# A graph layer's edge loop: 139 fetched columns and 15 fetched rows a chunk instead of 35 columns

## The chip, the cores and the metric

The kernel runs on one core of a Trainium2 chip. The metric is the device time of one execution in microseconds; the kernel before has a median of 4821.73 us over 3 runs.

## The reference

A message-passing layer on a graph of 12,500 nodes (48 values each) and 400,000 edges (32 values each), sorted by destination:

```python
h = jnp.maximum(_layernorm(x, axis=-1), 0.0)
x_i, x_j = h[dst], h[src]
tmp = jnp.concatenate([x_i, x_j, edge_attr], axis=1)      # 48 + 48 + 32
msg = jax.nn.relu(tmp @ W1 + b1) @ W2 + b2                # 128 hidden values
out = x + jax.ops.segment_sum(msg, dst, num_segments=12500)
```

## The kernel before, in words

**Tables.** W1 is split by its three inputs. A first stage (`node_tables`) makes the normalised nodes and from them two tables in DRAM of 12,500 rows of 128 values: `tab_a` (what a node gives as a destination, with the bias) and `tab_b` (what it gives as a source). `tab_b` is also kept transposed in SBUF as `bt`, 128 hidden values by nodes, so that one node's row is one column of `bt`.

**The edge loop** (`windows`) goes over 391 chunks of 1,024 edges, each eight tiles of 128 edges. Because the edges are sorted, a chunk's destinations lie in a window of 80 nodes, so the `tab_a` part and the edge part come from one matmul a tile: `rhs` holds the 80 table rows and 32 rows of W1, `lhs` the one-hot of the destinations and the edges' values (`before`, L400, into the PSUM tile `pre`). The source part has no such order and reaches the sum in one of two ways:

- *Gathered*: POOL issues one indirect DMA a tile (L373), which fetches 128 rows of `tab_b` into the tile `gb`. DVE adds `gb` to `pre` (L425).
- *Turned*: for some tiles, ACT and DVE copy 128 single columns of `bt` into a tile `gt` (L351), at addresses that they load into registers from a list of numbers (`last`); PE then adds `gt` transposed to `pre` by a matmul with the identity (`turned`, L409). 35 columns are copied a chunk (`PARTS`: 3 on DVE, 16 + 16 on ACT), so every 3.7 chunks one tile is complete.

`hidden` then makes the relu on ACT (L432, and L431 for a turned tile) into an SBUF tile `h`; `fold` multiplies `h` with the one-hot `hot` of the destinations (L440), and `add` accumulates the result in SBUF (L455). Every twelve chunks a segment is multiplied with W2 and stored.

**Order.** Each engine takes its instructions in the order in which the loop emits them: in iteration `c` the loads, the one-hots and the gathers of chunk `c` (`prepare`; rhs, lhs and row on SP's queue at L359, L364 and L366), then PE's `before` of chunk `c - 1`, `fold` of `c - 2` and `turned` of `c - 1`, then `hidden` of `c - 1` and `add` of `c - 2`, with the column copies of the parts in between. POOL runs ahead as far as buffers allow: `gb` has six (pool `gp`), and one is free again when DVE's add has read it. `pre` has two buffers in PSUM, `rhs` three in SBUF.

Of the kernel before, what the change touches and what calls it, by code (L numbers as in the profile page):

```python
# [8 lines left out]
F32 = mybir.dt.float32  # L9
I32 = mybir.dt.int32  # L10
AF = mybir.ActivationFunctionType
# [5 lines left out]
P = 128  # L17
N, D, DE, HID, E = 12500, 48, 32, 128, 400000
# [3 lines left out]
NT = E // P  # L22
T = 8
# [20 lines left out]
U8 = mybir.dt.uint8  # L44
# [3 lines left out]


COLS = 1  # L50
END = NT // T


PARTS = (
    (True, 0, 3, 1),
    (False, 3, 16, 4),
    (False, 19, 16, 20),
)
PART = sum(n for _, _, n, _ in PARTS)
BASE = 36  # L60
DVE_PARTS = sum(dve for dve, *_ in PARTS)
BEHIND = len(PARTS) - 1

BT0 = 16512
SEG0 = 121888
SEG_SIZE = 8 * L


SEG, NEXT, SEG2 = 40, 41, 42
PLACE0 = 43  # L70
WIDTH = 44
SLOTS = (NCH + 2 + P - 1) // P
MOST = 32

# [1 line left out]
def tiles_of(first, part):  # L76

    n = (END - first) * part // P
    return [first + (P * (j + 1) + part - 1) // part - 1 for j in range(n)]


BYCOLS = tiles_of(COLS, PART)
TURNED = {c: [j for j, of in enumerate(BYCOLS) if of == c] for c in set(BYCOLS)}


def turned_at(c):

    return ((), (T - 1,), (T // 2 - 1, T - 1))[len(TURNED.get(c, ()))]


def gathered_at(c):

    return [t for t in range(min(T, NT - c * T)) if t not in turned_at(c)]


EPS = 1e-5
# [8 lines left out]
def node_tables(nc, tc, keep, bt, x, ident, w1, b1, tab_a, tab_b, loads, most, check, rest):  # L105
# [5 lines left out]
    ta_v = tab_a[:NPAD, :].rearrange("(p r) h -> p r h", p=P)  # L111
    with ExitStack() as es:
        node = es.enter_context(tc.tile_pool(name="node", bufs=3))
        ps_t = es.enter_context(tc.tile_pool(name="ps_t", bufs=3, space=PSUM))
        ps_n = es.enter_context(tc.tile_pool(name="ps_n", bufs=3, space=PSUM))
        ps_s = es.enter_context(tc.tile_pool(name="ps_s", bufs=1, space=PSUM))
# [68 lines left out]
        def table(j, wt, tv, dve):  # L185

            r0, rb = slices[j]
            rows = wt.shape[0]
            t = node.tile([P, rb, HID], F32, name="tab")
            for g in range(0, rb // 2, 2):  # L190
                n = min(2, rb // 2 - g)
                p_n = ps_n.tile([P, 2, 2 * HID], F32, name="p_n")
                for q in range(n):
                    nc.tensor.matmul(
                        p_n[:, q, :], hts[j][:rows, g + q, :],
                        wt.rearrange("k a h -> k (a h)"), start=True, stop=True,
                    )
                to = t[:, 2 * g : 2 * (g + n), :].rearrange("p r h -> p (r h)")
                of = p_n[:, :n, :].rearrange("p q h -> p (q h)")
                if dve and g % 4:  # L200
                    nc.vector.tensor_copy(to, of)
                else:
                    nc.scalar.copy(to, of)
            nc.sync.dma_start(tv[:, r0 : r0 + rb, :], t)
# [43 lines left out]
def windows(nc, tc, gp, bt, ident, idx, x_t, tab_a, tab_b, dst, edge_t, w1, w2s, b2s, out_t):  # L248
# [3 lines left out]
    with ExitStack() as es:  # L252
# [19 lines left out]
        for _, _, n, at in PARTS:  # L272
# [1 line left out]
                last[:, :, at : at + n], last[:, :, at : at + n], 4, BT0,  # L274
                op0=ALU.mult, op1=ALU.add,
            )
        rows_at = slice(BASE, BASE + 1)
        nc.vector.tensor_scalar(
            last[:, :, rows_at], last[:, :, rows_at], 4 * HID, None, op0=ALU.mult
        )  # L280
        taba8 = tab_a.rearrange("n h -> (n h)").bitcast(U8)

        place = PARTS[0][3] - 1
        for a, b in ((place, SEG2), (NEXT, SEG)):
# [16 lines left out]
            rhss.append(rhs)  # L301
        st = {}
        gts = {}

        def group(c):

# [15 lines left out]

        def node(n):
            return n.with_bounds(min_val=0, max_val=N - 1)

        regs = {}

# [25 lines left out]
        def prepare(c):  # L353
            n = min(T, NT - c * T)
            at = c * CE
            base, = numbers(c, BASE, 1, mybir.EngineType.SP)
            rhs = rhss[c % 3]
            base = base.with_bounds(min_val=0, max_val=4 * HID * (N - 1))
            nc.sync.dma_start(  # L359
                rhs.bitcast(U8)[:W, :],  # L360
                taba8[bass.ds(base, 4 * HID * W)].rearrange("(w h) -> w h", w=W),
            )
            lhs = ld.tile([P, CE], F32, name="lhs")
            nc.sync.dma_start(lhs[W:K, : n * P], edge_t[:, at : at + n * P])  # L364
            row = ld.tile([W, CE], I16, name="row")
            nc.sync.dma_start(  # L366
                row[:, : n * P],
                dst[at : at + n * P].rearrange("(o e) -> o e", o=1).to_broadcast([W, n * P]),
            )
            st[c] = dict(n=n)  # L370
            gb = gp.tile([P, T, HID], F32, name="gb")
            for t in gathered_at(c):
                nc.gpsimd.indirect_dma_start(  # L373
                    out=gb[:, t, :], out_offset=None, in_=tab_b[:, :],
                    in_offset=bass.IndirectOffsetOnAxis(
                        ap=srci[:, c * T + t : c * T + t + 1], axis=0
                    ),
                )

            deg = degs[c % 3]  # L380
            nc.vector.tensor_scalar(  # L381
                lhs[:W, : n * P], row[:, : n * P], bw[:, c : c + 1], None,
                op0=ALU.is_equal, op1=ALU.add, accum_out=deg[:, :1],
            )
            load(c, 0)
            columns(c, 0)
            hot = wp.tile([P, T, W], F32, name="hot")
            nc.vector.tensor_tensor(  # L388
                hot[:, :n, :], wnum.unsqueeze(1).to_broadcast([P, n, W]),
                rel[:, c * T : c * T + n].unsqueeze(2).to_broadcast([P, n, W]), op=ALU.is_equal,  # L390
            )
            st[c].update(rhs=rhs, lhs=lhs, gb=gb, deg=deg, hot=hot)
# [18 lines left out]
        def hidden(c):  # L411
            s = st[c]
            n, pre = s["n"], s["pre"]
            h = wp.tile([P, T, HID], F32, name="hid")
            two = len(turned_at(c)) == 2
            half = T // 2

            def added(x, to):

                if not two:  # L420
                    return x[:, :to, :]
                return x.rearrange("p (b t) h -> p b t h", b=2)[:, :, : half - 1, :]

            to = n - len(turned_at(c))
            nc.vector.tensor_add(added(h, to), added(pre, to), added(s["gb"], to))  # L425
            if two:
                nc.scalar.activation(
                    h[:, half - 1 :: half, :], pre[:, half - 1 :: half, :], AF.Relu
                )
            elif to < n:  # L430
                nc.scalar.activation(h[:, to, :], pre[:, to, :], AF.Relu)  # L431
            nc.scalar.activation(added(h, to), added(h, to), AF.Relu)  # L432
            s["h"] = h

        def fold(c):
# [53 lines left out]
        with tc.manual_schedule():  # L489
            for c in range(NCH + 2):  # L490
                if c < NCH:
                    prepare(c)
                if c >= NCH:
                    load(c, 0)
                    columns(c, 0)
                for part in range(1, DVE_PARTS - 1):
                    load(c, part)
                    columns(c, part)
                if 0 <= c - 1 < NCH:
                    before(c - 1)  # L500
                if 0 <= c - 2 < NCH:
                    fold(c - 2)
                if 0 <= c - 1 < NCH:
                    turned(c - 1)

                g, k = group(c - 2)
                if k == GQ - 3 or c == NCH - 1:
                    segment_load(g)
                if g > 0 and k < L // BLK:
                    segment_sum(g - 1, k, BLK)  # L510
                if g > 0 and k == STORE:
                    segment_store(g - 1, L)
                columns(c, DVE_PARTS)
                for part in range(DVE_PARTS + 1, BEHIND):
                    load(c, part)
                    columns(c, part)
                if 0 <= c - 1 < NCH:
                    hidden(c - 1)
                if DVE_PARTS > 1:
                    load(c, DVE_PARTS - 1)  # L520
                for part in range(BEHIND, len(PARTS)):
                    load(c, part)
                    columns(c, part)
                load(c + 1, DVE_PARTS)
                if 0 <= c - 2 < NCH:
                    add(c - 2)
                    if k == GQ - 1:
                        segment_next(g)
                if DVE_PARTS > 1:
                    columns(c, DVE_PARTS - 1)  # L530
                if c == NCH + 1:
                    segment_sum(g, 0, END_L)
                    segment_store(g, END_L)

                if c < PIECES:
                    s = slice(c * PIECE, (c + 1) * PIECE)
                    nc.sync.dma_start(out_t[:, s], x_t[:, s])
# [126 lines left out]
def tile_gnn_preln(  # L664
# [27 lines left out]
    nc = tc.nc  # L692
# [28 lines left out]
    for k in range(3):  # L721
        deg = const.tile([W, P], F32, name=f"deg{k}")
        nc.gpsimd.memset(deg, 0.0)
        degs.append(deg)
    gp = ctx.enter_context(tc.tile_pool(name="gp", bufs=6))

    with tc.tile_pool(name="keep", bufs=1) as keep, tc.tile_pool(
        name="ps_c", bufs=1, space=PSUM
# [146 lines left out]
```

## Time and profile before

| | |
|---|---|
| median of 3 runs (4817.93 to 4830.65) | 4821.73 us |
| profiled execution, its own time | 4847.12 us |
| its span | 4845.3 us |
| mean granted TensorE clock | 0.614 |
| tiles gathered (L373) | 3,019 of 3,125 |
| columns copied on ACT, on DVE (L351) | 12,404, 1,164 |
| moved by DMA | 367.73 MB, 76 GB/s |

The profile is one execution. A group's row gives the source line, the engine, the operation, out<-in by the program's names with the shape, the count, then the busy time, the mean duration of one in ns, and the idle time of the engine just before these instructions with what ended most of it. "issue" is idle time that ended without any wait that the profile shows; "remote" is a release whose origin it does not show. In the timeline a row is a start, a duration, and a run of like instructions.

### The profile page before, as it was taken

The numbers are of one execution on the slowest core, as the hardware profiler recorded it, in microseconds if no ns is written. First come the engines' busy times: TensorE is split into PE (matmuls) and PEld (weight loads), VectorE is DVE, ScalarE is ACT, GpSimd is POOL, SyncE is SP. The second block draws the span as 40 slices with busy tenths as digits, with TensorE's granted clock in tenths as the row PEclk, the third lists the DMA queues.
The fourth block names the chain that finished last, engine by engine and source line by source line (L and its number), as shares of the span: only waits on it lengthen the run. The fifth ranks groups of instructions, "written<-read, shape, count | busy, mean of one in ns | idle before, by whom it ended". The sixth has DMA issues, their size and how long they took to land. (4 is left out here: it accounts for less than half of the span.)

```text
span 4845.3 us, 55629 instructions
## 1 busy us (share of the span) xinstructions
PE 2962.1 (61%) x14064; PEld 2628.5 (54%) x14064; DVE 1534.8 (32%) x3366; ACT 1944.3 (40%) x12976; POOL 2895.0 (60%) x3047
## 2 busy tenths in 40 slices
PE   5565565555667555665556757666566655665656
PEld 3555564455556555655555656555455555554545
DVE  4333323332333232333323333332233332323333
ACT  3344343443334343443443444343344343434443
POOL 5466565565656566665656666656666665656663
PEclk7756656666555655556656565655655566656566
DMA  3422222222222222222222222222222222222222
GB/s 123 145 72 75 75 71 72 73 73 72 75 68 77 72 73 71 76 73 71 76 71 73 77 73 75 73 71 75 73 72 76 72 74 72 76 69 76 74 71 60
DMA packets 199966, 367.73 MB, mean 76 GB/s; under 512 B 69362, under 2 KB 101636, under 8 KB 198356
## 3 DMA queue, kind: packets, MB, share of 16 engines
q0 software_dynamic: 96640, 198.07, 16.4%
q1 hardware_dynamic: 102736, 165.92, 11.5%
q8 instruction: 115, 1.88, 0.2%
q14 instruction: 215, 1.76, 0.1%
q10 hardware_dynamic: 260, 0.10, 0.0%
HBM read 344.35 MB, written 22.07 MB: 76 GB/s over the span
## 5 line engine op out<-in xcount | busy, mean ns | idle before, releaser
L373 POOL DMA_INDIRECT gb<-tab_b,srci x3019 | 2873.3, 952 | 1898.0 <-DVE seg L455 953.0
L351 ACT COPY gt<-bt 128x1 f32 x12404 | 1495.6, 188 | 1985.4 <-issue 1957.3
L400 PE MATMUL pre<-rhs,lhs 112*128 112x128 f32 x6250 | 1357.6, 386 | 866.3 <-issue 655.1
L400 PEld LDWEIGHTS pre<-rhs,lhs 112*128 112x128 f32 x6250 | 1240.2, 292 | 1052.9 <-issue 849.9
L440 PE MATMUL p_g<-hot,hid 128*128 128x80 f32 x6250 | 1210.5, 366 | 691.2 <-ACT hid L432 312.9
L440 PEld LDWEIGHTS p_g<-hot,hid 128*128 128x128 f32 x6250 | 1156.3, 280 | 742.8 <-ACT hid L432 351.3
L425 DVE TENSOR_TENSOR hid<-pre,gb 128x1024 f32<-128x1024 f32 (+1 forms) x391 | 461.4, 1180 | 1727.0 <-issue 1357.5
L432 ACT ACTIVATE hid<-hid 128x1024 f32<-128x1024 f32 (+1 forms) x391 | 400.3, 1024 | 423.3 <-DVE hid L425 318.2
L381 DVE TENSOR_SCALAR_CACHE_REDUCE lhs<-row,bw 80x1024 f32<-80x1024 int16 x391 | 495.4, 1267 | 9.3 <-DMA row<-in_dst 9.3
L455 DVE TENSOR_TENSOR seg<-seg,p_g 128x160 f32 x391 | 122.4, 313 | 977.1 <-remote 824.1
L388 DVE TENSOR_TENSOR hot<-wnum,rel 128x640 f32<-128x640 f32 x391 | 316.1, 809 | 0.0
L443 PE MATMUL p_g<-ident,deg 80*128 80x80 f32 x782 | 213.4, 356 | 139.1 <-issue 138.8
L443 PEld LDWEIGHTS p_g<-ident,deg 80*128 80x128 f32 x782 | 181.1, 278 | 111.8 <-issue 111.4
L483 DVE TENSOR_TENSOR xseg<-xseg,p_f 48x512 f32<-48x512 f32 (+1 forms) x67 | 45.3, 676 | 497.6 <-remote 291.2
L431 ACT ACTIVATE hid<-pre 128x128 f32<-128x128 f32 x106 | 29.4, 278 | 390.0 <-DVE hid L425 273.8
L409 PE MATMUL pre<-ident,gt 128*128 128x128 f32 x212 | 70.1, 399 | 106.0 <-issue 96.1
L409 PEld LDWEIGHTS pre<-ident,gt 128*128 128x128 f32 x212 | 51.7, 282 | 108.8 <-issue 98.5
L482 PE MATMUL p_f<-seg,b2s 1*48 1x512 f32 (+1 forms) x134 | 98.0, 810 | 11.8 <-issue 11.8
L481 PE MATMUL p_f<-seg,w2s 128*48 128x512 f32 (+1 forms) x134 | 98.0, 815 | 11.3 <-issue 10.0
L351 DVE COPY gt<-bt 128x1 f32 x1164 | 103.0, 141 | 0.0
L482 PEld LDWEIGHTS p_f<-seg,b2s 1*48 1x48 f32 x134 | 13.4, 139 | 92.7 <-issue 91.8
L471 DVE MEMSET seg<- 128x944 f32 x64 | 54.1, 845 | 9.3
(66 smaller groups left out, 327.3 us busy)
## 6 DMA issues: line engine op xcount, KB each, us to landing
row<-in_dst SPq DMA_DIRECT2D x390, 160.0 KB
lhs<-in_edge_t SPq DMA_DIRECT2D x390, 128.0 KB
gb<-tab_b,srci POOLq DMA_INDIRECT x3019
rhs<-tab_a SPq DMA_DIRECT2D x391, 40.0 KB
xseg<-in_x_t SPq DMA_DIRECT2D x33, 192.0 KB
out_x<-xseg SPq DMA_DIRECT2D x33, 192.0 KB
tab_b<-tab SPq DMA_DIRECT2D x3, 1280.0 KB
tab_a<-tab SPq DMA_DIRECT2D x3, 1280.0 KB
```

What stands on the lines that cost most here:

```text
L351: copy(gts[of][:, e : e + 1], bt8[:, bass.ds(at, 4)].bitcast(F32))
L373: nc.gpsimd.indirect_dma_start(out=gb[:, t, :], out_offset=None, in_=tab_b[:, :], in_offset=bass.IndirectOffsetOnAxis(ap=srci[:, c * T + t ...
L381: nc.vector.tensor_scalar(lhs[:W, : n * P], row[:, : n * P], bw[:, c : c + 1], None, op0=ALU.is_equal, op1=ALU.add, accum_out=deg[:, :1],)
L388: nc.vector.tensor_tensor(hot[:, :n, :], wnum.unsqueeze(1).to_broadcast([P, n, W]), rel[:, c * T : c * T + n].unsqueeze(2).to_broadcast([P ...
L400: nc.tensor.matmul(pre[:, t, :], s["lhs"][:K, t * P : (t + 1) * P], s["rhs"][:K, :], start=True, stop=t not in turned_at(c),)
L409: nc.tensor.matmul(st[c]["pre"][:, t, :], gts.pop(j), ident, start=False, stop=True)
L425: nc.vector.tensor_add(added(h, to), added(pre, to), added(s["gb"], to))
L432: nc.scalar.activation(added(h, to), added(h, to), AF.Relu)
L440: nc.tensor.matmul(p_g[:, 0, :], s["h"][:, t, :], s["hot"][:, t, :], start=t == 0, stop=t == n - 1)
L443: nc.tensor.matmul(p_g[:, 1, :], s["deg"], ident[:W, :W], start=True, stop=True)
L455: nc.vector.tensor_add(to, to, s["p_g"])
L482: nc.tensor.matmul(p_f[:, :n], b2s[:1, :], seg[:1, 1, s], start=False, stop=True)
```

## The change

- **Columns**: 139 a chunk instead of 35: 63 on DVE (15 + 16 + 16 + 16) and 76 on ACT (16 x 4 + 12), with one load of registers for each group of at most sixteen. About one tile a chunk is turned instead of one in 3.7 chunks; a chunk can have two.
- **Rows**: SP fetches 15 rows of `tab_b` a chunk by DMAs of one row each into a tile `gs`, at addresses from registers. Every 8.5 chunks one tile is complete, and its chunk's DVE add reads `gs` for that tile instead of `gb`. Tiles that are turned or come by rows are not gathered by POOL.
- **The hidden tile**: DVE adds into `pre` in PSUM, and ACT's relu reads all of `pre` from there in one instruction, where DVE wrote to `h` in SBUF and ACT worked in place.
- **Buffers**: eight `gb` tiles instead of six; two buffers for the tables' tile `tab` instead of three.

```diff
 PARTS = (
-    (True, 0, 3, 1),
-    (False, 3, 16, 4),
-    (False, 19, 16, 20),
+    (True, 0, 15, 1),
+    (True, 15, 16, 16),
+    (True, 31, 16, 32),
+    (True, 47, 16, 48),
+    (False, 63, 16, 64),
+    (False, 79, 16, 80),
+    (False, 95, 16, 96),
+    (False, 111, 16, 112),
+    (False, 127, 12, 128),
 )
...
-BASE = 36
+BASE = 140
+RPART = 15
 DVE_PARTS = sum(dve for dve, *_ in PARTS)
-BEHIND = len(PARTS) - 1
+BEHIND = len(PARTS) - 2
...
+BYROWS = tiles_of(ROWS0, RPART)
...
+def single_at(c):
+
+    return (T - 2 if c in TURNED else T - 1) if c in BYROWS else None
+
+
 def gathered_at(c):
 
-    return [t for t in range(min(T, NT - c * T)) if t not in turned_at(c)]
+    return [t for t in range(min(T, NT - c * T)) if t not in turned_at(c) and t != single_at(c)]
...
         node = es.enter_context(tc.tile_pool(name="node", bufs=3))
+        tabs = es.enter_context(tc.tile_pool(name="tabs", bufs=2))
...
-            t = node.tile([P, rb, HID], F32, name="tab")
+            t = tabs.tile([P, rb, HID], F32, name="tab")
...
+        def rows(c, nodes):
+
+            for k, n in enumerate(nodes):
+                e = (c - ROWS0) * RPART + k
+                of = BYROWS[e // P]
+                if of not in gss:
+                    gss[of] = gtp.tile([P, HID], F32, name="gs")
+                n = n.with_bounds(min_val=0, max_val=4 * HID * (N - 1))
+                nc.sync.dma_start(
+                    gss[of].bitcast(U8)[e % P : e % P + 1, :],
+                    tab8[bass.ds(n, 4 * HID)].rearrange("(o h) -> o h", o=1),
+                )
...
-            base, = numbers(c, BASE, 1, mybir.EngineType.SP)
+            m = max(0, min(RPART, len(BYROWS) * P - (c - ROWS0) * RPART)) if c >= ROWS0 else 0
+            base, *nodes = numbers(c, BASE, 1 + m, mybir.EngineType.SP)
...
-            h = wp.tile([P, T, HID], F32, name="hid")
...
-            nc.vector.tensor_add(added(h, to), added(pre, to), added(s["gb"], to))
-            if two:
-                nc.scalar.activation(
-                    h[:, half - 1 :: half, :], pre[:, half - 1 :: half, :], AF.Relu
-                )
-            elif to < n:
-                nc.scalar.activation(h[:, to, :], pre[:, to, :], AF.Relu)
-            nc.scalar.activation(added(h, to), added(h, to), AF.Relu)
+            at = single_at(c)
+            if at is None:
+                parts = [(added(pre, to), added(s["gb"], to))]
+            else:
+                runs = [(0, half - 1), (half, at)] if two else [(0, at)]
+                parts = [(pre[:, a:b, :], s["gb"][:, a:b, :]) for a, b in runs]
+                parts.append((pre[:, at, :], gss.pop(c)))
+            for of, rows in parts:
+                nc.vector.tensor_add(of, of, rows)
+            h = wp.tile([P, T, HID], F32, name="hid")
+            nc.scalar.activation(h[:, :n, :], pre[:, :n, :], AF.Relu)
...
                 if c < NCH:
                     prepare(c)
+                    rows(c, st[c].pop("rows"))
...
-    gp = ctx.enter_context(tc.tile_pool(name="gp", bufs=6))
+    gp = ctx.enter_context(tc.tile_pool(name="gp", bufs=8))
```

More of the change, by code (lines that the diff above doesn't have):

```diff
@@ L50 @@
 COLS = 1
+ROWS0 = 1
 END = NT // T
 PARTS = (
-    (True, 0, 3, 1),
-    (False, 3, 16, 4),
-    (False, 19, 16, 20),
+    (True, 0, 15, 1),
[7 more added lines that the diff above has]
+    (False, 127, 12, 128),
 )
 PART = sum(n for _, _, n, _ in PARTS)
-BASE = 36
+BASE = 140
+RPART = 15
 DVE_PARTS = sum(dve for dve, *_ in PARTS)
-BEHIND = len(PARTS) - 1
+BEHIND = len(PARTS) - 2
 BT0 = 16512
-SEG0 = 121888
+SEG0 = 131936
 SEG_SIZE = 8 * L
-SEG, NEXT, SEG2 = 40, 41, 42
-PLACE0 = 43
-WIDTH = 44
+SEG, NEXT, SEG2 = 156, 157, 158
+PLACE0 = 159
+WIDTH = 160
 SLOTS = (NCH + 2 + P - 1) // P
@@ L276, in windows @@
             )
-        rows_at = slice(BASE, BASE + 1)
+        rows_at = slice(BASE, BASE + 1 + RPART)
         nc.vector.tensor_scalar(
@@ L280, in windows @@
         )
-        taba8 = tab_a.rearrange("n h -> (n h)").bitcast(U8)
+        tab8, taba8 = (t.rearrange("n h -> (n h)").bitcast(U8) for t in (tab_b, tab_a))
         place = PARTS[0][3] - 1
@@ L303, in windows @@
         gts = {}
+        gss = {}
         def group(c):
@@ L369, in prepare @@
             )
-            st[c] = dict(n=n)
+            st[c] = dict(n=n, rows=nodes)
             gb = gp.tile([P, T, HID], F32, name="gb")
@@ L839 @@
         numbers[COLS : COLS + len(cols), at : at + n] = cols[:, k : k + n]
+    in_rows = [c * T + single_at(c) for c in BYROWS]
+    rows = by_tile[in_rows].reshape(-1)
+    rows = np.pad(rows, (0, -len(rows) % RPART)).reshape(-1, RPART)
+    numbers[ROWS0 : ROWS0 + len(rows), BASE + 1 : BASE + 1 + RPART] = rows
     last = np.ascontiguousarray(numbers.reshape(SLOTS, P, WIDTH).transpose(1, 0, 2))
```

## The prediction

> **What bounds the kernel now.** I read the page first: its busy times, its chain of waits and its costliest groups.
>
> ```profile
> span 4845.3 us, 55629 instructions
> PE 2962.1 (61%) x14064; PEld 2628.5 (54%) x14064; DVE 1534.8 (32%) x3366; ACT 1944.3 (40%) x12976; POOL 2895.0 (60%) x3047
> ...
> issue 6%; PE 6%; another core or an unknown queue 3%; DVE 2%; ACT 1%; DVEq 0%; POOL 0%; DMA 0%; ACTq 0%
> ...
> L373 POOL DMA_INDIRECT gb<-tab_b,srci x3019 | 2873.3, 952 | 1898.0 <-DVE seg L455 953.0
> L351 ACT COPY gt<-bt 128x1 f32 x12404 | 1495.6, 188 | 1985.4 <-issue 1957.3
> ...
> L425 DVE TENSOR_TENSOR hid<-pre,gb 128x1024 f32<-128x1024 f32 (+1 forms) x391 | 461.4, 1180 | 1727.0 <-issue 1357.5
> L432 ACT ACTIVATE hid<-hid 128x1024 f32<-128x1024 f32 (+1 forms) x391 | 400.3, 1024 | 423.3 <-DVE hid L425 318.2
> L381 DVE TENSOR_SCALAR_CACHE_REDUCE lhs<-row,bw 80x1024 f32<-80x1024 int16 x391 | 495.4, 1267 | 9.3 <-DMA row<-in_dst 9.3
> L455 DVE TENSOR_TENSOR seg<-seg,p_g 128x160 f32 x391 | 122.4, 313 | 977.1 <-remote 824.1
> L388 DVE TENSOR_TENSOR hot<-wnum,rel 128x640 f32<-128x640 f32 x391 | 316.1, 809 | 0.0
> ...
> L351 DVE COPY gt<-bt 128x1 f32 x1164 | 103.0, 141 | 0.0
> ```
>
> No engine is full (61% at most), and the chain of waits names almost nothing: its largest part is "issue", time in which an engine had nothing to wait for. So the bound is a state, not an instruction. The waits of POOL say how its two kinds of idle time divide:
>
> ```profile
> POOL gb L373 <- DVE seg L455: 953.0, 217, 8.9
> POOL gb L373 <- issue: 855.9, 2762, 1.7
> ```
>
> Between gathers lies 855.9 / 2762 = 0.31 us, so POOL works at 0.952 + 0.31 = 1.26 us a gather, 3,810 us in all; 217 times it stops, 953.0 / 217 = 4.4 us each. 391 chunks over 217 stops are 1.8 chunks a run. The "seg" named is DVE's work just behind the add L425, which frees a gb buffer: POOL stops because all six are full.
>
> Then the timeline over one such cycle:
>
> ```profile
> 2024.19 0.33 SPq L359 DMA_DIRECT2D rhs<-tab_a  x1
> ...
> 2024.62 0.37 SPq L364 DMA_DIRECT2D lhs<-in_edge_t  x1
> 2025.04 0.41 SPq L366 DMA_DIRECT2D row<-in_dst  x1
> ...
> 2025.78 0.95 POOL L373 DMA_INDIRECT gb<-tab_b,srci  x1 [4.55 <-DVE seg L455]
> 2026.66 2.93 ACT L351 COPY gt<-bt 128x1 f32 x29
> ...
> 2026.85 0.27 DVE L351 COPY gt<-bt 128x1 f32 x3
> 2027.03 0.94 POOL L373 DMA_INDIRECT gb<-tab_b,srci  x1 [0.30 <-issue]
> ...
> 2030.04 0.38 ACT L351 COPY gt<-bt 128x1 f32 x3 [0.44 <-issue]
> ...
> 2030.63 3.70 PE L400 MATMUL pre<-rhs,lhs 112*128 112x128 f32 x16
> ...
> 2043.29 0.95 POOL L373 DMA_INDIRECT gb<-tab_b,srci  x1 [0.30 <-issue]
> 2043.53 0.37 PE L400 MATMUL pre<-rhs,lhs 112*128 112x128 f32 x1 [1.73 <-issue]
> 2044.20 0.19 ACT L351 COPY gt<-bt 128x1 f32 x1 [0.51 <-issue]
> ...
> 2047.01 0.93 ACT L351 COPY gt<-bt 128x1 f32 x9 [0.50 <-issue]
> ...
> 2048.72 0.94 POOL L373 DMA_INDIRECT gb<-tab_b,srci  x1 [4.48 <-DVE seg L455]
> ```
>
> At 2026.66 ACT makes 29 copies in 2.93 us, 0.101 us each. From 2030.04 on, 4.3 us after POOL's restart, it starts single copies with half a microsecond of "issue" before each, and PE does the same a little later (2043.53: one matmul after 1.73 us of nothing). It ends at 2047.01, 2.8 us after POOL's last gather ended (2043.29 + 0.95). The table by stretches counts it:
>
> ```profile
> core 0: us, PE busy (x) PEld busy (x) DVE busy (x) ACT busy (x) POOL busy (x), PEclk, DMA share, GB/s
> ...
> 2024.00:2030.00 6.00, 5.93 (x29) 5.93 (x28) 4.56 (x9) 5.21 (x43) 3.31 (x4) 0.50 0.39 112
> 2030.00:2036.00 6.00, 6.00 (x32) 6.00 (x32) 2.43 (x7) 2.85 (x15) 4.47 (x6) 0.55 0.28 79
> 2036.00:2047.00 11.00, 2.71 (x13) 2.04 (x12) 0.00 (x0) 2.29 (x12) 6.41 (x7) 0.63 0.19 48
> ```
>
> ACT begins 43 instructions in 6 us, then 15 + 12 = 27 in the 17 us in which gathers are under way. DVE is not seen to crawl here, but only because it has nothing to do. At the start, with no edge loop yet, it is held as well:
>
> ```profile
> 102.28 0.69 DVE L201 COPY tab<-p_n 128x512 f32<-128x512 f32 x1 [20.88 <-remote]
> ...
> 109.71 0.94 POOL L373 DMA_INDIRECT gb<-tab_b,srci  x1 [0.31 <-issue]
> 113.49 0.59 ACT L203 COPY tab<-p_n 128x512 f32<-128x512 f32 x1 [21.84 <-remote]
> ...
> 119.24 10.96 PE L194 MATMUL p_n<-wa,ht 97*128 97x256 f32 x39 [3.04 <-DVE tab L201]
> ```
>
> The signals come 20 us late, until 2.8 us after the gather at 109.71 ended; then the tables run through, to 130.2 us. So **POOL's running and the other engines' working largely exclude one another**, and a chunk costs the held time (POOL's run) plus the others' work that is left. What the hold is made of the trace does not say. [...]
>
> **The change, part by part.** Turned tiles: 389 x 139 / 128 = 422 instead of 389 x 35 / 128 = 106; tiles by rows: 389 x 15 / 128 = 45. Gathers: 3125 - 422 - 45 = 2658, 361 fewer. At 1.26 us that takes 455 us off POOL: 3,355 us, 8.6 us a chunk instead of 9.7.
>
> *ACT*, undisturbed, a chunk: 76 copies x 0.101 = 7.7 us (before 32, 3.2); the relu 1.02 (L432). It now reads PSUM; L431, which does that already for one tile, bounds the difference:
>
> ```profile
> L431 ACT ACTIVATE hid<-pre 128x128 f32<-128x128 f32 x106 | 29.4, 278 | 390.0 <-DVE hid L425 273.8
> ...
> L409 PE MATMUL pre<-ident,gt 128*128 128x128 f32 x212 | 70.1, 399 | 106.0 <-issue 96.1
> ```
>
> L431 itself goes (0.08 us a chunk), and I take the large one as unchanged, within 0.1 us either way. Five register loads of sixteen instead of two: each between nothing and the 0.44 us of idle time behind the 29 copies; 1.1 us for five, bounds 0 and 2.2. Sum 9.8 us (8.6 to 11.0), against 4.8 now.
>
> *DVE*: 1.27 + 0.81 + 1.18 + 0.31 = 3.6 us stay; 63 copies at 0.09 in a run of three (0.27 / 3), less in a long run (0.141 is one, so (0.27 - 0.141) / 2 = 0.065 each further): 4.1 to 5.7; four loads, 0 to 1.8. About 9.2 us (7.7 to 11.1), from 3.9. It becomes a second ACT, not a worse one.
>
> *SP*: 15 single-row loads a chunk behind rhs, lhs and row of the same chunk. Issues follow at 0.42 us (2024.19, 2024.62, 2025.04): 18 x 0.42 = 7.6 us and one longer load of numbers. No row shows a DMA of one row; from 0.33 (L359's issue) up to the rival below. Queued behind them are the next chunk's rhs, lhs and row, for which PE and DVE wait. Cover: SP is up to three chunks ahead (three rhs buffers), as long as 18 issues fit into a chunk.
>
> *PE*: 16 + 16 + 2 + 2 x 422 / 391 = 36.2 matmuls at 3.70 / 16 = 0.23 us (the turned ones, L409, taken like L400: their mean of 399 ns is pipelined time too): 8.4 us. Under ACT.
>
> *In PSUM*: the pre tile is free only when ACT's relu has read it, not when DVE has added. PE's `before` of two chunks later waits for it; PE's fold of the chunk in between already waits for a later relu, so it costs nothing; uncovered it would be one relu, 1.0 us a chunk. *Eight buffers*: about ten more gathers run ahead at the start, while the tables are held: 12 us later. *Two tab tiles*: a store more to wait for, 0 to 15 us, I take 5.
>
> **The sum.** A run of POOL holds the others for its length less 1.5 us (2.8 after its end, 4.3 free at its start), and in it ACT starts 27 / 17 = 1.6 instructions a us. With one chunk a run: held 8.6 - 1.5 = 7.1 us, 11 copies (1.1 us) done in it, 9.8 - 1.1 = 8.7 left: 15.8 us a chunk. With two: held 15.7, 25 copies, 17.1 left: 32.8, 16.4 a chunk. The same rule for the kernel before, two chunks: 19.5 - 1.5 = 18.0 held, 29 copies, 9.6 - 2.9 = 6.7 left: 12.35 a chunk, where (4845.3 - 130.2) / 391 = 12.06 is measured: it overstates by 2.4%. Corrected: 15.4 to 16.0, I take 15.7. 391 x 15.7 = 6139, and 130 + 12 + 5 before the loop: 6,286 us. The profiled execution took 4847.12 against a median of 4821.73, 0.5% more: **6,250 us**. With ACT's bounds (8.6, 11.0) the same way (mean of one and two chunks a run, 14.5 and 16.9 us): 5,800 to 6,700.
>
> **The rivals.**
>
> *The hold dissolves (faster).* Runs of 6.8 gathers end 8.6 us after they begin; if the hold needs the long runs of now (16 gathers) to build up, it vanishes, POOL never waits, and the slowest engine decides: ACT, 9.8 us. 391 x 9.8 + 147 = 3,980, about 3,960 us. Deciding point: less than 12.06 - 9.8 = 2.3 us held a chunk. For it: 4.3 us of every run are free. Against: at 1.8 chunks a run some runs of now are already short ones, and 217 stops still cost 953 us; with POOL running 8.6 of 9.8 us there would be no pause of 2.8 us to clear it. 9%.
>
> *Half of it.* The hold begins later, since fewer large loads fall into a run: 3.6 us a chunk; 3.6 + 9.2 = 12.8, 391 x 12.8 + 147, near 5,130 us. 13%.
>
> *SP becomes the bound.* If the issues of single rows are held like ACT's copies, or cost over (15.7 - 7.1) / 18 = 0.48 us, SP's chunk is the longest: at 0.6 us 18 x 0.6 + 7.1 = 17.9 us, 7,100 us; at 1 us far more. For it: 15 new DMAs and their semaphores; against: nothing now waits on SP's issues. 11%.
>
> *DVE's copies stretch POOL.* If POOL could not make descriptors while DVE copies, 60 more copies at 0.065 to 0.09 would lengthen its run by 3.9 to 5.4 us a chunk, to some 13.2: held 11.7, 19 copies (1.9 us) done in it, 7.9 left, 19.6, corrected 19.1 us a chunk, 7,600 us. Against: the gather at 2027.03 overlaps DVE's copies and took 0.94, like the others. 3%. [...]
>
> **How the numbers follow.** Forecast 64%: 6,250. The range reaches down over most of "half of it" and up over SP at 0.6 us: 5,000 to 7,200; outside are the dissolved hold, dearer SP issues and the port. What can be told from no change is about 0.3%. Faster: the first rival and a little of the second, 10%; within 0.3%: 1%; slower 89%.
>
> **What would show it.** Right: POOL's waits for buffers grow from 953 us to some 2,700 (6,250 less 3,355 and the start), in nearly 390 stops instead of 217, at an unchanged 0.95 and 0.31 a gather; ACT's copies near 29,500 with "issue" still the largest part of their idle time; DVE's copies with "issue" before them, which they do not have now. Wrong: POOL idle under 5% (the hold is gone), SP's issues spaced over 0.5 us with DVE or PE waiting for row or lhs (SP), or gathers longer than 1.0 us (port).

## The result, and the profile after

The changed kernel takes 5261.82 us (median of 4 runs, 5259.14 to 5266.54), the kernel before, beside it, 4826.19 us: a ratio of 1.0905 [1.0884, 1.0926]. Slower, as forecast, but by 436 us where the forecast said some 1,430. And the experiments found something larger than either number: on other occasions the same two kernels take 3,527 and 3,856 us, and there the change is a gain.

The changed kernel's page: span, busy times, chain, and the three groups that matter (count, busy, mean ns, then the idle time just before and what ended most of it).

```profile
span 5264.8 us, 110310 instructions
...
PE 3215.1 (61%) x14696; PEld 2890.8 (55%) x14696; DVE 3164.5 (60%) x26769; ACT 3496.5 (66%) x29975; POOL 2551.4 (48%) x2686
...
ACT 59%; issue 30%; ACTq 4%; PE 2%; DVE 1%; DVEq 0%; POOL 0%; DMA 0%; another core or an unknown queue 0%
...
L380 ACT COPY gt<-bt 128x1 f32 x29509 | 3121.5, 187 | 1594.3 <-issue 1565.9
L403 POOL DMA_INDIRECT gb<-tab_b,srci x2658 | 2529.8, 952 | 2627.4 <-DVE pre L462 1334.9
L380 DVE COPY gt<-bt 128x1 f32 x24507 | 1820.2, 143 | 1661.1 <-issue 1653.0
```

The pattern of before has stayed: no engine is full, and ACT's idle time ends in "issue". DVE now shows it too. The chain that named almost nothing before now consists of ACT (59%) and "issue" (30%). POOL's waits:

```profile
POOL gb L403 <- DVE pre L462: 1334.9, 248, 52.8
POOL gb L403 <- issue: 694.9, 2274, 0.6
POOL gb L403 <- DVE seg L487: 563.7, 133, 13.5
```

It waits for buffers 1334.9 + 563.7 = 1,898.6 us in 248 + 133 = 381 stops: about one stop a chunk. One cycle in the timeline (start, duration, a run of like instructions):

```profile
2508.71 0.94 POOL L403 DMA_INDIRECT gb<-tab_b,srci  x1 [3.49 <-DVE pre L462]
...
2511.39 9.18 SPq L350 DMA_DIRECT2D gs<-tab_b  x15
2512.15 0.28 ACT L380 COPY gt<-bt 128x1 f32 x2 [0.22 <-issue]
...
2514.30 0.38 ACT L380 COPY gt<-bt 128x1 f32 x3 [1.04 <-issue]
...
2516.20 0.94 POOL L403 DMA_INDIRECT gb<-tab_b,srci  x1 [0.30 <-issue]
...
2518.60 1.02 ACT L464 ACTIVATE hid<-pre 128x1024 f32<-128x1024 f32 x1 [0.52 <-issue]
2519.52 7.54 ACT L380 COPY gt<-bt 128x1 f32 x76
...
2525.77 0.94 POOL L403 DMA_INDIRECT gb<-tab_b,srci  x1 [8.64 <-DVE pre L462]
```

POOL restarts at 2508.71; from 2512.15, 3.4 us later, ACT starts copies in twos and threes with a pause of up to 1.1 us before each; POOL's last gather of the run ends at 2517.14; at 2518.60, 1.5 us later, ACT is free, and the relu and all 76 copies, register loads included, run through in 8.5 us. POOL stands still until 2525.77. (This cycle of 17.1 us is a long one; the mean is 13.1.)

### The profile page after: what moved, and what is told of

It is laid out like the page before. It is cut to its first block, busy times and chain, and to the rows that moved or that the text cites. A ratio compares the mean times of both kernels' runs of the same rounds, so it can differ in the third digit from the quotient of the medians.

```text
span 5264.8 us, 110310 instructions
## 1 busy us (share of the span) xinstructions
PE 3215.1 (61%) x14696; PEld 2890.8 (55%) x14696; DVE 3164.5 (60%) x26769; ACT 3496.5 (66%) x29975; POOL 2551.4 (48%) x2686
## 2 busy tenths in 40 slices
DMA packets 200357, 350.77 MB, mean 67 GB/s; under 512 B 69346, under 2 KB 107252, under 8 KB 198324
## 4 chain that ended last, share of the span: by engine, by line
ACT 59%; issue 30%; ACTq 4%; PE 2%; DVE 1%; DVEq 0%; POOL 0%; DMA 0%; another core or an unknown queue 0%
ACT gt L380 53%; ACT hid L464 7%; ACTq L332 4%; PE p_g L472 1%; DVE gt L380 1%; PE p_f L514 0%; PE p_f L513 0%; DVEq L332 0%; DVE pre L462 0%; DVE lhs L411 0%; PE pre L439 0%; POOL gb L403 0%; DVE hot L418 0%; PE p_g L475 0%; DMA gb<-tab_b,srci 0%
## 5 line engine op out<-in xcount | busy, mean ns | idle before, releaser
L380 ACT COPY gt<-bt 128x1 f32 x29509 | 3121.5, 187 | 1594.3 <-issue 1565.9
L403 POOL DMA_INDIRECT gb<-tab_b,srci x2658 | 2529.8, 952 | 2627.4 <-DVE pre L462 1334.9
L380 DVE COPY gt<-bt 128x1 f32 x24507 | 1820.2, 143 | 1661.1 <-issue 1653.0
L472 PE MATMUL p_g<-hot,hid 128*128 128x80 f32 x6250 | 1351.9, 405 | 1887.7 <-ACT hid L464 891.0
L472 PEld LDWEIGHTS p_g<-hot,hid 128*128 128x128 f32 x6250 | 1274.0, 311 | 1977.0 <-ACT hid L464 938.0
L430 PE MATMUL pre<-rhs,lhs 112*128 112x128 f32 x6250 | 1265.4, 388 | 15.7 <-DMA lhs<-in_edge_t 15.7
L462 DVE TENSOR_TENSOR pre<-pre,gb 128x896 f32<-128x896 f32 (+4 forms) x400 | 417.6, 1044 | 166.7 <-issue 133.1
L464 ACT ACTIVATE hid<-pre 128x1024 f32<-128x1024 f32 x391 | 396.0, 1013 | 59.4 <-DVE pre L462 37.8
L439 PE MATMUL pre<-ident,gt 128*128 128x128 f32 x844 | 289.7, 446 | 77.4 <-ACT gt L380 31.4
L439 PEld LDWEIGHTS pre<-ident,gt 128*128 128x128 f32 x844 | 216.7, 315 | 88.0 <-ACT gt L380 41.1
```

The lines of the kernel that those rows point to most:

```text
L380: copy(gts[of][:, e : e + 1], bt8[:, bass.ds(at, 4)].bitcast(F32))
L403: nc.gpsimd.indirect_dma_start(out=gb[:, t, :], out_offset=None, in_=tab_b[:, :], in_offset=bass.IndirectOffsetOnAxis(ap=srci[:, c * T + t ...
L430: nc.tensor.matmul(pre[:, t, :], s["lhs"][:K, t * P : (t + 1) * P], s["rhs"][:K, :], start=True, stop=t not in turned_at(c),)
L439: nc.tensor.matmul(st[c]["pre"][:, t, :], gts.pop(j), ident, start=False, stop=True)
L462: nc.vector.tensor_add(of, of, rows)
L464: nc.scalar.activation(h[:, :n, :], pre[:, :n, :], AF.Relu)
```

## The experiments

Two readings had to be told apart: the engines are *held* while POOL's gathers run, whatever is in the kernel, or the change makes a wait of its own. In the text "with the hold" is a place where the kernel before takes about 4,830 us, "without" one where it takes about 3,850 us. A place is one chip on one occasion: chip 4 stands on both sides, without the hold in e1 to e6 and with it in e11 to e14. All ratios are to the kernel before at the same place.

**e1: no gathers.** A POOL memset of `gb` takes the gathers' place; the gathered part of the sum is missing.

```diff
-            for t in gathered_at(c):
-                nc.gpsimd.indirect_dma_start(out=gb[:, t, :], ..., in_=tab_b[:, :], ...)
+            nc.gpsimd.memset(gb, 0.0)
```

> The kernel after with POOL's gathers left out: one memset of the whole gb tile a chunk stands in their place, so the gathered part of the sum is missing. Theory A (POOL's runs of gathers hold ACT, DVE and PE; a chunk is the held time plus what ACT has left): without gathers nothing is held, and ACT alone decides: 76 copies at 0.097 and one relu of 1.02, 8.4 us a chunk, 3,400 us; with 0.2 us for each of five register loads 3,800. Theory B (the chain of ACT, PE and DVE is that long by itself, gathers or not): within 5% of the kernel after, over 5,000 us.

3532.47 us (one run), between the theory's 3,400 and 3,800, with ACT 93% busy. But the kernel before took 3847.54 us in the same place, so this shows ACT's limit and not yet the hold's cause.

**e2: the columns of before**; rows, relu from PSUM and buffers as changed. (The edit also sets `BEHIND`, the first part that is copied behind the relu, back to `len(PARTS) - 1`; so do e4 and e14.)

```diff
-    (True, 0, 15, 1), ... (False, 127, 12, 128),
+    (True, 0, 3, 1),
+    (False, 3, 16, 16),
+    (False, 19, 16, 32),
```

> The kernel after with the columns alone undone: 35 a chunk again (3 on DVE, 16 and 16 on ACT); rows, relu from PSUM, eight and two buffers stay. Theory A: the columns are the whole loss; 2,974 gathers instead of the 3,019 of the kernel before take 45 x 1.26 = 57 us off POOL, near 4,770 us, not over 4,850. Theory C (rows, PSUM or buffers cost part of the loss): over 4,900 us.

**e3: no rows**; columns, relu from PSUM and buffers as changed.

```diff
-RPART = 15
+RPART = 0
```

> The kernel after with the rows alone undone: 45 tiles more are gathered by POOL (2,703), SP issues no single-row loads. Theory A: 45 x 1.26 = 57 us more of POOL's run and as much more held time: 5,320 us. Theory C (the 5,760 single-row loads themselves slow SP or lengthen the hold): faster than the kernel after, under 5,230 us.

**e4: 31 columns on DVE, 32 on ACT**, 15 rows.

```diff
+    (True, 0, 15, 1),
+    (True, 15, 16, 16),
+    (False, 31, 16, 64),
+    (False, 47, 16, 80),
```

> The kernel after with 63 columns a chunk: 31 on DVE (15 and 16) and 32 on ACT (16 and 16), 15 rows. 191 tiles turned, 45 by rows, 2,889 gathered. Theory A with ACT as the only engine whose work counts: ACT's work is that of the kernel before, DVE's 28 more copies lie beside it, and 130 gathers fewer than in the kernel before take 0.42 us a chunk off: 4,660 us. Rival: DVE's copies cost like ACT's, some 28 x 0.07 = 2.0 us a chunk less the 0.42: 5,430 us.

The three expectations for times were made for a place with the hold and are all missed: 3790.48 us (0.9851 [0.9834, 0.9867]), 3521.77 us (0.9144 [0.9119, 0.9169]) and 3688.69 us (0.9586 [0.957, 0.9602]). What they show is the kernel without the hold. In e2 POOL runs without a stop:

```profile
POOL 59%; issue 29%; DMA 5%; PE 3%; SPq 3%; DVE 1%; ACT 0%; DVEq 0%; POOLq 0%; ACTq 0%
...
L397 POOL DMA_INDIRECT gb<-tab_b,srci x2974 | 2812.5, 946 | 926.4 <-issue 889.9
```

2974 gathers at 0.946 + 889.9 / 2918 = 1.251 us are 3,720 of 3,789 us: POOL is the bound, and each gather less is worth 1.25 us, until ACT's copies become the bound (e3: ACT busy 93%).

**e5: the changed kernel, unaltered,** in such a place.

> The changed kernel, unaltered. Theory C (the hold of ACT, PE and DVE under POOL's runs of gathers belongs to the place where the kernel runs and not to its code): where the kernel before takes 3,848 us there is no hold, POOL needs 2658 gathers x 1.25 us + 147 = 3,470 us and ACT about 391 x 8.5 + 147 = 3,470 us, so about 3,500 us, a ratio near 0.91, with POOL waiting for pre under 10% and ACT over 90% busy; where the kernel before takes 4,826 us, 5,262 us again, a ratio of 1.09. Theory D (the rows bring a hold of their own, since they are what the runs so far left out or paired with fewer columns): over 4,500 us even where the kernel before takes 3,848 us, with POOL waiting for pre in over 300 stops.

3527.11 us, 0.9148 [0.9132, 0.9163]: the change is a gain of 8.5% there, and the rows add nothing to the columns (e3: 0.9144).

```profile
span 3532.5 us, 110310 instructions
...
PE 2700.1 (76%) x14696; PEld 2421.2 (69%) x14696; DVE 2972.8 (84%) x26769; ACT 3267.4 (92%) x29975; POOL 2548.3 (72%) x2686
...
L403 POOL DMA_INDIRECT gb<-tab_b,srci x2658 | 2526.7, 951 | 901.1 <-issue 741.0
L380 ACT COPY gt<-bt 128x1 f32 x29509 | 2885.8, 188 | 75.2 <-issue 35.0
```

The instruction counts are the same as above to the last one, the gathers last as long (951 and 952 ns), and 1,566 us of "issue" ahead of ACT's copies are 35. In its timeline ACT makes its 76 copies, and SP its 15 rows, while POOL's gathers follow each other:

```profile
2500.33 0.94 POOL L403 DMA_INDIRECT gb<-tab_b,srci  x1 [0.30 <-issue]
2501.25 4.91 SPq L350 DMA_DIRECT2D gs<-tab_b  x15
2501.58 0.95 POOL L403 DMA_INDIRECT gb<-tab_b,srci  x1 [0.31 <-issue]
2502.05 7.53 ACT L380 COPY gt<-bt 128x1 f32 x76
```

**e6: each gather as two of 64 rows,** twice POOL's instructions; the second takes the indices of the first, so half the rows are the wrong ones.

```diff
+                for p in (0, P // 2):
+                    nc.gpsimd.indirect_dma_start(out=gb[p : p + P // 2, t, :], ...)
```

> Each gather is split into two gathers of 64 rows, the second with the indices of the first half, so the same bytes come with twice POOL's instructions and the rows of the second half are the wrong ones. Theory C, where there is no hold: POOL is the bound, 5316 gathers at some 0.7 to 1.0 us with what lies between, 3,900 to 5,400 us, and ACT's copies are not held (mean wait before a copy under 0.02 us). Rival (the hold is set off by how densely POOL issues gathers, and the changed code only passes a threshold): ACT shows single starts of 0.5 us and more while the runs are under way, and the idle time that ends with issue before ACT's copies is over 1,000 us.

```profile
L404 POOL DMA_INDIRECT gb<-tab_b,srci x5316 | 4808.5, 905 | 1641.4 <-issue 1561.0
...
L380 ACT COPY gt<-bt 128x1 f32 x29509 | 2891.5, 187 | 106.9 <-issue 40.8
```

6497.16 us (one run), above what was expected: half the rows cost POOL 0.905 instead of 0.951 us, so it is mostly a price for the instruction. There is no hold: 40.8 us of "issue" ahead of ACT's copies. Without the hold, gathers 1.21 us apart instead of 1.25 do not set it off; each brings half the rows, so denser rows were not tried.

**e7: six `gb` buffers again.**

```diff
-    gp = ctx.enter_context(tc.tile_pool(name="gp", bufs=8))
+    gp = ctx.enter_context(tc.tile_pool(name="gp", bufs=6))
```

> Six buffers of gathered rows again instead of eight, all else as changed. Theory C: where there is no hold the turned copies keep pace and POOL hardly waits, so two more buffers are worth little: 3,527 to 3,600 us (ratio 0.915 to 0.935; POOL's waits for pre and seg under 300 us). Where the kernel before takes 4,826 us: within 2% of 5,262 us, since POOL's stops are set by ACT's remaining work and not by the reserve. Rival (the eight buffers carry the gain): above 3,700 us with POOL waiting for pre over 400 us.

3531.79 us, 0.917 [0.9155, 0.9186] without the hold: the two buffers are worth next to nothing there.

**e8: DVE 71 and ACT 72 columns.**

```diff
+    (True, 63, 8, 64),
-    (False, 127, 12, 128),
+    (False, 135, 8, 136),
```

> DVE 71 and ACT 72 columns a chunk instead of 63 and 76, 15 rows as before: four copies less for ACT (0.39 us), eight more for DVE (0.52 us), 12 gathers fewer. In the unheld profile of the changed kernel POOL waits 901 us ahead of 2658 gathers, 741 of it issue, and ACT is busy 92%: both are at their limit. Theory C: ACT's limit falls to about 3,380 us and POOL's is 2646 x 1.256 + 160 = 3,480 us, so 3,470 to 3,500 us, a ratio of 0.900 to 0.908. Rival (DVE, 84% busy, becomes late, at some 8.1 us a chunk plus its waits): 3,550 us and more.

```profile
DVE 55%; issue 14%; DMA 6%; POOL 6%; SPq 6%; PE 5%; DVEq 4%; ACT 1%; ACTq 0%; POOLq 0%
```

3788.54 us, 0.9842 [0.9826, 0.9858]: the rival of the expectation. DVE carries 55% of the chain, not ACT; "issue" ahead of its copies has doubled (239 us in e5, 496 here), beside a fifth load of registers. So DVE's room ends somewhere from 63 to 71 columns.

**e9: the gathers' bytes by one plain DMA a chunk on SP** (eight contiguous tiles: the wrong rows).

```diff
-            for t in gathered_at(c): nc.gpsimd.indirect_dma_start(...)
+            nc.sync.dma_start(gb, tab_b[: T * P, :].rearrange("(t p) h -> p t h", p=P))
```

> The chunk's gathers are replaced by one plain DMA of eight contiguous tiles of the table, issued by SP, so the same number of bytes (and some more) comes without POOL; the added rows are the wrong ones. Theory C, where there is no hold: ACT is the bound as without gathers, 3,500 to 3,600 us. Where the kernel before takes 4,826 us it tells the hold's cause: about 3,600 us if the hold comes with POOL's descriptors, over 5,000 us if it comes with the bytes into the buffers.

4055.96 us (one run), more than expected: DVE's compare now waits 600 us for the int16 row (1.91 and 1.87 us ahead of the two compares in its timeline from 2500 to 2518 us), which SP loads on the same queue as the large DMA. A baseline for e12.

**e10: ACT 72 columns, SP 18 rows.** This ran in a place with the hold (before: 4829.93 us).

```diff
-    (False, 127, 12, 128),
+    (False, 127, 8, 128),
-RPART = 15
+RPART = 18
```

> ACT 72 columns a chunk instead of 76, DVE 63 as changed, 18 rows instead of 15: work moves from ACT to SP, the number of gathers stays (some 2,660). Theory C: where there is no hold ACT goes from 8.4 to 8.0 us a chunk and POOL alone is the limit, 2,660 x 1.256 + 160 = 3,500 us, so 3,480 to 3,520 us, a ratio of 0.903 to 0.915, no more than 1% from the changed kernel's 0.9148; SP needs some 18 x 0.35 + 1.2 = 7.5 us of 8.6 and the loads of its registers, and should it be late after all, 3,600 us and more. Where the kernel before takes 4,826 us: four copies fewer outside the hold take 0.4 us off a chunk, about 5,100 us, a ratio of 1.06.

5415.02 us, 1.1215 [1.1189, 1.1241]: missed, slower than the change. Its page, then its timeline:

```profile
L411 DVE TENSOR_SCALAR_CACHE_REDUCE lhs<-row,bw 80x1024 f32<-80x1024 int16 x391 | 498.1, 1274 | 1485.2 <-DMA row<-in_dst 1167.9
```

```profile
2509.22 10.66 SPq L350 DMA_DIRECT2D gs<-tab_b  x18
```

SP is held like the others: 18 rows in 10.66 us, 0.59 each (9.8 us in the median of all chunks), and behind them comes the next chunk's int16 row, for which DVE's compare now waits 1,168 us.

**e11 and e12: e1 and e9 again, with the hold** (before: 4831.06 us).

> The changed kernel with a memset in place of POOL's gathers (the gathered part of the sum is missing), as e1, for a place where the kernel before takes 4,826 us. Theory E (the hold needs POOL's software gathers under way): ACT is not held, 3,500 to 3,600 us, as the 3,532 us of e1. Rival F (there every instruction start is slow, whatever POOL does; the gathers only fall into it): over 4,500 us, with issue ahead of ACT's copies still above 1,000 us.

> One plain DMA of SP brings eight contiguous tiles in place of a chunk's gathers (the added rows are the wrong ones), as e9, for a place where the kernel before takes 4,826 us. If the hold comes with POOL's own descriptors: about 4,056 us, as e9. If it comes with the bytes or the DMA engines' work: over 5,000 us with issue ahead of ACT's copies above 1,000 us.

3518.68 and 4054.74 us (one run each), the times of e1 and e9. e11's page, then e12's:

```profile
span 3517.0 us, 106539 instructions
...
PE 2683.2 (76%) x14696; PEld 2412.1 (69%) x14696; DVE 2957.5 (84%) x26769; ACT 3266.2 (93%) x29975; POOL 393.1 (11%) x419
...
L380 ACT COPY gt<-bt 128x1 f32 x29509 | 2885.7, 188 | 71.6 <-issue 38.6
```

```profile
q1 hardware_dynamic: 520896, 374.15, 32.8%
...
L380 ACT COPY gt<-bt 128x1 f32 x29509 | 2891.0, 187 | 103.2 <-issue 39.9
```

38.6 and 39.9 us of "issue" against 1,565.9: without POOL's gathers there is no hold, and more bytes in more packets by plain DMAs (374.15 MB in 520,896 on q1, against 350.77 MB in 200,357 on all queues of the changed kernel) make none. The hold needs POOL's gathers, and a place that has it. The granted clock is not what tells the places apart: it is 0.742 in e1 and 0.740 in e11.

**e13 and e14: e3 and e2 again, with the hold.**

> The columns and buffers of the change without its rows, as e3 (0.9144 of the kernel before where there is no hold). Where the kernel before takes 4,826 us: theory E says ACT sets the pace with 5.9 us held and the rest free, as in the changed kernel, so the same pause and 45 gathers more at most, 5,262 to 5,400 us, a ratio of 1.09 to 1.12. Rival G (SP is held too, its rows stretch from 5.2 to 9.2 us a chunk, and the next chunk's int16 row waits behind them): without the rows the chunk starts earlier, under 5,150 us, a ratio below 1.07.

> The rows and buffers of the change with the columns of the kernel before, as e2 (0.9851 where there is no hold). Where the kernel before takes 4,826 us: theory E, ACT's 32 copies, POOL's runs as before with 45 fewer gathers: 4,700 to 4,830 us, a ratio of 0.975 to 1.00. Rival G (SP held and late): above 4,900 us, with DVE's compare waiting for the int16 row.

e13 5134.91 us, 1.0623 [1.058, 1.0667]; e14 5642.24 us, 1.1682 [1.1631, 1.1732]. The change without its rows costs 6% there, without its new columns 17%. (Relu from PSUM and buffers are in both; they were not tried alone with the hold.) Both times the rival with a held SP is right, in e14 strongly (its page, then its timeline):

```profile
L405 DVE TENSOR_SCALAR_CACHE_REDUCE lhs<-row,bw 80x1024 f32<-80x1024 int16 x391 | 498.1, 1274 | 3405.0 <-DMA row<-in_dst 3141.0
```

```profile
2520.16 19.15 SPq L344 DMA_DIRECT2D gs<-tab_b  x15
```

In the long run of POOL shown (two chunks) 15 rows take 19 us; in the median of all chunks they take 9.4. In the changed kernel itself the compare waits 7.6 us in all: one chunk a run leaves SP just enough time (9.2 us of 13.1), and e10's three rows more are over the edge.

**e15 to e18: wider spacing of the gathers,** with the hold. A memset of a scratch tile on POOL ahead of each gather; 256, 768, 512 and 384 elements a partition.

```diff
             for t in gathered_at(c):
+                nc.gpsimd.memset(pause, 0.0)
                 nc.gpsimd.indirect_dma_start(
```

> The changed kernel with a POOL memset of a scratch tile (256 elements a partition, some 0.3 us by the 951 ns that 1024 took in e1) ahead of each gather: 1.25 us from gather to gather become some 1.55. Where there is no hold POOL is the bound: 2658 x 1.55 + 147 = 4,270 us, 4,150 to 4,450. Where the kernel before takes 4,826 us: theory H (POOL's gathers leave a backlog that is worked off at a fixed rate, the hold is that backlog) says that the wider spacing shrinks or ends the hold, 4,270 to 4,700 us, less than the kernel before. Rival I (each gather holds the other engines while POOL works on it, whatever the spacing): the runs grow from 8.2 to 10.3 us and the hold with them, 5.9 to 8.0 us, so some 15 us a chunk, 5,700 to 6,100 us.

> The same with 768 elements a partition, some 0.75 us: 2.0 us from gather to gather. No hold, or theory H with it: POOL is the bound, 2658 x 2.0 + 147 = 5,460 us, 5,300 to 5,700. Rival I: the runs grow to 13 us, the hold to 11 us a chunk, over 6,200 us.

> Between e15 and e16: a memset of 512 elements, some 0.54 us, so about 1.65 us from gather to gather (e16: 1.87 us with one of 0.755). Theory H, where the hold exists: it is gone or nearly, POOL is the bound, 2658 x 1.65 + 116 = 4,500 us, up to 4,700 with a rest of the hold, a ratio of 0.93 to 0.97, below both kernels. Against it: a hold that needs a spacing close to e16's 1.87 us leaves 4,850 us and more. Where there is no hold: 4,500 us.

> A memset of 384 elements, some 0.43 us, so about 1.54 us from gather to gather. Theory H with a backlog of about 1.5 us a gather (the runs of the changed kernel: held from 3.8 us after the first gather to 1.5 us after the end of the last, in runs of 8.2 us with seven gathers, so 4 w = 8.2 + 1.5 - 3.8): the hold is all but gone, 2658 x 1.54 + 116 = 4,210 us, up to 4,500. If the work behind a gather is longer, 1.6 us and over: a rest of the hold, 4,500 to 4,950 us. Where there is no hold: 4,210 us.

| from gather to gather | run | time, ratio | "issue" ahead of ACT's copies | POOL's waits for pre and seg |
|---|---|---|---|---|
| 1.25 us | changed kernel | 5261.82 us, 1.0905 | 1565.9 us | 1,898.6 us |
| 1.44 us | e15 | 4952.49 us, 1.023 [1.0197, 1.0264] | 1256.6 us | 985.6 us |
| 1.55 us | e18 | 4621.93 us, 0.9523 [0.9497, 0.9549] | 878.2 us | 352.4 us |
| 1.66 us | e17 | 4527.21 us, 0.9326 [0.9304, 0.9349] | 46.6 us | none |
| 1.87 us | e16 | 5088.32 us (one run) | 40.5 us | none |

The rows of ACT's copies in e15, e18 and e16:

```profile
L381 ACT COPY gt<-bt 128x1 f32 x29509 | 3160.4, 188 | 1291.3 <-issue 1256.6
L381 ACT COPY gt<-bt 128x1 f32 x29509 | 3143.5, 188 | 952.5 <-issue 878.2
L381 ACT COPY gt<-bt 128x1 f32 x29509 | 2891.8, 187 | 106.6 <-issue 40.5
```

More work for POOL makes the kernel faster, until the hold is gone; from there on POOL is the bound and the time rises again. e17's page, with its chain:

```profile
POOL 83%; issue 10%; DVE 3%; PE 2%; DMA 1%; ACT 0%; DVEq 0%; SPq 0%; POOLq 0%; ACTq 0%
...
L405 POOL DMA_INDIRECT gb<-tab_b,srci x2658 | 2536.6, 954 | 445.6 <-issue 442.7
L404 POOL MEMSET pause<- 128x512 f32 x2658 | 1440.3, 542 | 62.1 <-ACT tab L218 60.1
...
L381 ACT COPY gt<-bt 128x1 f32 x29509 | 2895.9, 187 | 114.4 <-issue 46.6
```

e15 lies between what the two expected, nearer to the backlog's 4,700 us, but not below the kernel before as that theory had said; e16 was to come at 2.0 us a gather and came at 1.87, since with a memset in it only 0.17 us of the gap of 0.31 is left. The rival that each gather holds the others for as long as POOL works on it is refuted: it wanted 5,700 us and more of e15. e18 met the second of its two cases, a rest of the hold at 1.55 us. e17, where the hold is, beats both kernels. Without the hold it was not run; by POOL's 2658 x 1.66 = 4,410 us alone it would be slower there than both.

## Why the prediction was right and wrong

*Right, and shown.* The mechanism, for a place with the hold: held while POOL's gathers run, the rest of the work after them. POOL's gathers unchanged at 0.952 us and 694.9 / 2274 = 0.31 between them; 381 stops where nearly 390 were forecast; 29,509 copies on ACT with "issue" as almost all of their idle time; the same ahead of DVE's. POOL's waits came to 1,898.6 us and not to some 2,700, which follows from the two terms below. e11 and e12 show that the held time comes with POOL's gathers and not with bytes.

*Wrong: two terms of the sum.* The forecast was 7.1 us held, 11 copies done in it, 9.8 us of ACT's work: 15.8 us a chunk. Measured as means over the some 370 one-chunk runs of the trace (six or seven gathers each): 5.9 us held (a run is 8.2 us; the hold begins 3.8 us after its start and ends 1.5 us after its last gather), 11.6 copies done in it, 2.0 a us (1.8 to 2.5 by the pause that counts) where the forecast had 1.6; ACT's work is 3266.2 / 391 = 8.4 us (e11). 5.9 + 8.4 - 1.1 = 13.2, and the run shows 13.1. The held time depends on how long a pause must be to count: with 0.1 to 0.4 us it is 4.6 to 6.2 us with 8 to 14 copies, and the sum 12.2 to 13.2. So:

1. "A run of POOL holds the others for its length less 1.5 us" took both ends, the 4.3 us free and the 2.8 us of tail, from one run of sixteen gathers, and gave them no bounds. Measured are a tail shorter by 1.3, a run shorter by 0.4 (8.2 us, not 8.6) and a free start shorter by 0.5: 1.2 us a chunk too much.
2. "Five register loads ... 1.1 us for five", of 0 to 2.2: the 76 copies with their loads take 7.5 us at a stretch, 0.099 a copy; the loads hide behind the copies. That and the price of a copy: 1.4 us too much. The 8.4 us lie under the prediction's own lower bound of 8.6.

2.6 us x 391 = 1,017 us; the forecast was 6,250 - 5,262 = 988 us too high. The check of the rule on the kernel before (12.35 against 12.06) could not see this: there ACT has little work, and most runs are long.

*Half of it.* Its 5,130 us lie nearer to 5,262 than the forecast does, by luck: it set 3.6 us held and 9.2 us of work left, where 5.9 and 7.3 were measured, and the hold begins no later in a run than before (3.8 us, not 4.3).

*SP becomes the bound.* The reason against it, that nothing waits on SP now, was true of the kernel before but did not carry over: SP's issues are held, 15 in 9.18 us, 0.61 each, over the 0.48 at which the rival was to begin. It did not decide because 18 issues at up to 0.61 us, 11 us, still fit into a chunk of 13.1; the rival had put the 7.1 us held on top of them. e10 and e14 show it deciding. Even so the rows cost 5262 - 5135 = 127 us with the hold (e13) and gain nothing without it.

*The hold dissolves.* The case that had 9%, ACT at the limit and POOL hardly waiting, is what happens without the hold, at 3,527 us and not 3,960 (again the 8.4 us). The prediction took the hold for a property of the kernel and looked for its end in the length of the runs. It ends with the place, and with the spacing of the gathers: between 1.55 and 1.66 us it goes.

*DVE's copies stretch POOL* ("the port" in the forecast's range and signs). With 24,507 copies on DVE the gathers took 952 ns, the same as with 1,164 in the kernel before, so no stretch shows.

*Open.* What the hold is made of: no run here shows it; every run on record comes with a core's span and clock, so whether the hold is there when nothing is recorded is open too. What decides that a place has the hold. The runs' records name chips 4 and 6 for the places without it and 14, 4, 5 and 10 for those with it, so the number alone does not. A backlog behind each gather is not seen either: if there is one, its work is near 1.6 us a gather, an estimate from e18 and e17 (878.2 us of "issue" ahead of ACT's copies at 1.55 us, 46.6 at 1.66), but a backlog of that size does not explain why short runs of the kernel before have tails of 3.3 us and those of the changed kernel 1.5 (medians of the time from a run's last gather to ACT's next stretch of copies). Since those short runs have long tails, the shorter runs are not shown to be why the tail came out at 1.5. That the memset helps by the spacing alone, and not by being a memset, was not separated; nor was what relu from PSUM and the buffers cost with the hold.

## What to carry to other kernels

Where several engines show "issue" before single instructions at the same moments, measure the kernel before on more than one chip and occasion before sizing a change: here the sign depends on it. Where one engine's dense work holds up the others, try slowing it: with the hold 0.41 us of delay a gather was worth 14% of the changed kernel's time. And a rule read from one run of sixteen gathers needs bounds of its own when the change makes runs of seven; the short runs of the kernel before, with tails of 3.3 us, would have shown that the ends vary, though not that they come to 1.5.

## What the hardware showed

One program, two steady times: medians of 4,822 to 4,855 us and of 3,848 to 3,856 us for the kernel before, each within 1% over all its runs. Where the hold exists it strikes ACT, DVE, PE and SP, not POOL: "issue" ahead of the copies of the changed kernel is 1,565.9 us on ACT and 1,653.0 on DVE, against 35.0 and 239 without the hold (e5), and 655.1 us ahead of PE's matmuls L400 in the kernel before; POOL's gathers take 952 ns with it and 951 without. The hold begins some 4 us after the first gather of a run (3.6 to 4.6 by the run and the pause that counts) and ends 1.4 to 3.3 us after the last (kernel before, changed kernel, e10, e13), and it is gone at 1.66 us from gather to gather (e17: 46.6 us of "issue" ahead of ACT's copies). An indirect gather of 64 rows costs POOL 0.905 us (e6), one of 128 rows 0.951 (e5). Loads of single rows from SP take 0.33 us each without the hold (15 in 4.91, e5) and 0.61 with it (15 in 9.18).
